# Two attention layers on one core: the order of small work around the projection streams

## The chip, the cores and the metric

The kernel runs on one core of a Trainium2 chip. The metric is the device time of one execution in microseconds (us), smaller is better. The engines are called TensorE (PE in the profile, PEld for its weight loads), VectorE (DVE), ScalarE (ACT), GpSimd (POOL) and SyncE (SP, which only issues transfers here). They run side by side; each takes its own instructions in order and waits for the others through semaphores.

## What is computed

Two layers, one after the other, on 8 images of 512 channels and 32 x 32 pixels, in float32. Cut to what matters:

```python
def layer(x, gn_w, gn_b, qkv_w, qkv_b, proj_w, proj_b, groups):   # groups: 8, then 32
    xn = group_norm(x, groups) * gn_w + gn_b
    q, k, v = split(einsum('oc,bcn->bon', qkv_w, xn) + qkv_b)     # 8 heads of 64
    attn = softmax(einsum('bhdi,bhdj->bhij', q, k) / 8)
    out = einsum('bhij,bhdj->bhdi', attn, v)
    return einsum('oc,bcn->bon', proj_w, out) + proj_b + x
```

## The kernel before

The work is cut into 16 **units**: unit u = 0 to 7 is layer 0 on image u, unit 8 to 15 is layer 1. In every unit two kinds of stage alternate.

**Projection streams.** A projection multiplies a 512 x 512 weight matrix with the 512 x 1024 image. It is done by a seven-product scheme in place of eight block products, on two levels: seven outer products k, in the order `ORDER = (1, 6, 2, 7, 5, 4, 3)` (L50), and in each of them seven inner **parts** j. The operands of the products are sums and differences of blocks, which have to be made first; the code calls this mixing. On the weights' side it is `mix_left` (L175): four operations on rows of 512 (outer) and four on 7 x 128 = 896 (inner). On the image's side it is `Right.mix`, `quarter` and `single` (L217 to L249). Weight mixtures are made once for each layer, stored as images in DRAM (`store_image`, L190) and loaded for each unit (`load_image`, L195).

`Stream.product` (L422) issues one outer product. Its parts 1, 6 and 5 accumulate into one small PSUM region called `one`; between them ScalarE copies that region to the main bank pair as a start value (`seed`, L443). So part 6 may only start when the copy behind part 1 has read `one`, part 5 when the copy behind part 6 has, and part 3 when the copy behind part 5 has written its quarter. Parts 4 and 3 are kept back as a **tail** and issued after part 1 of the next product. In steady state TensorE therefore runs 1', 4, 3, 6', 2', 7', 5', 1'', ... (dashes: the next products), and every copy has two parts to hide behind. The first product of a stream has no tail before it; there (`alone`, L449) part 7 is issued right behind part 1.

When a product is complete, `finish` **takes** it: VectorE adds the main bank pair to sums in SBUF, GpSimd adds the seventh part (`late`). The main pairs alternate, so the take of product n must be done before product n+2 can be seeded. After the take, `hook(sel, k)` runs whatever has been hung there with `at(sel, k, ...)` (L1011): mixing, loads, and work left over from the unit before. With "v,7" I mean the hook behind the take of product 7 of the v stream.

From unit 1 on a unit runs the streams v, q, k and then o (the output projection of the unit before). Work of the unit before that hangs in them: the transposed and reduced softmax sums of its last chunk (v,1 and v,2), their `reciprocals` (L894: five small VectorE operations, a transfer to DRAM and two broadcast transfers back), `divide` (L916), `add_bias` (L923), and the mixing of the attention output for the o stream (`ro.mix` and `o_part`, L1112). `o_part(5, ...)` and `o_part(1, ...)` run on VectorE, `o_part(2, ...)` and `o_part(4, ...)` on GpSimd.

Unit 0 makes v with full products (`make_values`, L697) and has no o stream. Beside its q and k streams VectorE mixes the first layer's weights as they arrive; those of o are `outer_o` and `inner_o` (L1091).

**Attention** (L782). 64 steps s, 8 chunks c of 8 steps t. In a step TensorE makes scores (L815, 8 records), ScalarE exponentiates them (L823), and the products with v of the step before follow (L843). VectorE adds up the exponentials (`summed`, L860). At t = 0 the chunk before is evacuated (a ScalarE copy L869, a VectorE add L870) and its sums transposed (L875), at t = 2 reduced (L883). The exponentials have five buffers. `at_step` (L1211) hangs the next unit's normalisation in the steps, by the tables USUAL and LATE (unit 0): statistics of x, means and variances (`norm`: small TensorE products into the other chunk's bank, read back by VectorE; the products of that chunk wait for the read-back through `free`), the scales, and their application on ScalarE (`apply`, which waits for the scales). `making` (L1220) mixes one weight matrix of layer 1 in each of units 1 to 4 on VectorE, two operations in each of chunks 1 to 4. `shadows` (L1249) are GpSimd operations that are made to follow a given sum[...].

Of the kernel before, what the change touches and what calls it, by code (L numbers as in the profile page):

```python
# [32 lines left out]
def fast_path(ctx, tc, x, qkv_wT, proj_wT, vecs, groups, out, flag):  # L33
# [5 lines left out]
    nc = tc.nc  # L39
# [3 lines left out]
    NT = N // P  # L43
# [367 lines left out]
    class Stream:  # L411


        def __init__(self, first):
            self.n, self.tail = first, None
# [6 lines left out]
        def product(self, a, b, keep, finish, tokens=False):  # L422
# [6 lines left out]
            def part(j, dst, tile_name, bank, start=False):  # L429
# [19 lines left out]
            alone = self.tail is None  # L449

            def apart():
                part(7, seventh, s, 1, not keep)

            def kept():
                on("ACT", nc.scalar.copy(late, seventh), s, 1)  # L455

            part(1, one, s, 0, True)
            if alone:
                apart()
            seed(q11, 0)  # L460
            if alone:
                kept()
# [4 lines left out]
            if not alone:  # L467
                apart()
                kept()
# [119 lines left out]
    def stream_values(stream, w, left, hook):  # L589
# [32 lines left out]
        for k in ORDER:  # L622

            def finish(main, m, late, k=k):
                steps[k](main, m, late)
                hook("v", k)

            stream.product(left.quarters(k), w.right.inner[k], k == 3, finish, True)
# [350 lines left out]
    def first_weights(after):  # L979
# [17 lines left out]
        "stats": (4, 5, 6, 7, 10, 11, 12, 13), "norm": (15, 20, 27, 30),  # L997
        "apply": (32, 33, 36, 38, 39, 41, 43, 44),
    }
    MAKE = {1: (1, "v"), 2: (1, "q"), 3: (1, "k"), 4: (1, "o")}  # L1000

    old = None
    for u in range(2 * B):
# [59 lines left out]
        if u == 0:  # L1063
# [28 lines left out]
            at("k", 2, partial(run, outer_o[:2]))  # L1092
            at("k", 7, partial(run, outer_o[2:]))
            at("k", 4, partial(run, inner_o[:2]))
            at("k", 3, partial(run, inner_o[2:]), partial(store_image, 0, "o", slot_q))
        else:
# [21 lines left out]
            at("v", 7, reciprocals)  # L1118
            at("v", 4, bias_2[0])
            at("v", 3, bias_2[1], o_rooms, partial(ro.mix, 0))  # L1120
            at("q", 1, divide)
            at("q", 6, bias[0])
            at("q", 2, bias[1])
            at("q", 7, partial(ro.mix, 1), o_part(2, 0, 1))
            at("q", 5, o_part(2, 1, 2))
            at("q", 4, partial(ro.mix, 3))
            at("q", 3, partial(ro.mix, 2))
            at("k", 1, o_part(1, 0, 2))
            at("k", 6, o_part(1, 2), o_part(2, 2, 3))
            at("k", 2, o_part(5, 0, 2), o_part(2, 3))  # L1130
# [405 lines left out]
```

## Time and profile before

| | us |
|---|---|
| three runs, median (lowest to highest) | 3202.29 (3200.21 to 3202.36) |
| the profiled execution: its time, its span from first to last instruction | 3201.04, 3199.3 |
| TensorE busy | 3174.4 (99%) |
| VectorE, ScalarE, GpSimd busy | 2682.8, 2045.5, 1223.6 |
| start of unit 0's attention, length of that attention | 88.08, 110.74 |
| unit 7: v stream; q, k and o streams; attention | 22.19, 64.72, 110.26 |
| v stream of units 1, 2, 4, 5 | 24.86, 22.56, 22.89, 22.85 |
| attention of units 1, 2, 3, 4 | 112.19, 111.36, 111.36, 111.35 |

The stage lengths are read from TensorE's timeline: from the first matmul of a stage to the first of the next one. A stream of v starts with the first matmul of 128 rows by 128 x 128 behind an attention, a q stream with the first of 128 x 256.

A timeline row has start, duration, engine, line, operation, output <- inputs, shape and count; what stands in brackets is how long the engine sat idle before it and what ended that. Neighbouring instructions of the same kind are merged (x4). Since matmuls are pipelined and their ends are modelled, this document measures TensorE from start to start.

### The profile page before, as it was taken

How to read it: one execution, taken by the hardware profiler on the slowest of the kernel's cores; microseconds unless marked ns; L12 is line 12 of the kernel's file. 1: busy time of each engine (PE TensorE's matmuls, PEld its weight loads, DVE VectorE, ACT ScalarE, POOL GpSimd, SP SyncE). 2: the span in 40 equal slices, each digit the busy share in tenths (PEclk: the TensorE clock that was granted, in tenths of full speed). 3: DMA queues.
4: the chain of work that ended last, by engine and by line, in shares of the span. 5: the costliest groups of instructions: out<-in, count | busy, mean ns of one | idle time of the engine just before them, and what ended most of it. 6: DMA issues, size and time to landing. Idle time of an engine off the chain costs nothing.

```text
span 3199.3 us, 63763 instructions
## 1 busy us (share of the span) xinstructions
PE 3174.4 (99%) x24272; PEld 2031.5 (63%) x24272; DVE 2682.8 (84%) x3172; ACT 2045.5 (64%) x3572; POOL 1223.6 (38%) x945
## 2 busy tenths in 40 slices
PE   9999999999999999999999999999999999999999
PEld 7466485664846659476584765847567485674843
DVE  7987978879788797887979879788797988879777
ACT  3665767667666676766667666676666766667664
POOL 4235171451714417154270533605336162351620
PEclk9999999999999999999999999999999999999999
DMA  4334342443424324243242331423314333243311
GB/s 173 108 120 136 118 141 88 167 137 115 150 81 169 120 74 148 82 130 120 63 161 79 119 127 56 167 79 122 119 58 165 90 127 102 83 149 91 131 62 49
DMA packets 155268, 365.78 MB, mean 114 GB/s; under 512 B 30160, under 2 KB 45776, under 8 KB 154960
## 3 DMA queue, kind: packets, MB, share of 16 engines
q1 hardware_dynamic: 154672, 361.53, 34.5%
q8 instruction: 195, 3.19, 0.4%
q14 instruction: 113, 0.93, 0.1%
q10 hardware_dynamic: 288, 0.13, 0.0%
HBM read 299.72 MB, written 59.77 MB: 112 GB/s over the span
## 4 chain that ended last, share of the span: by engine, by line
PE 85%; DVE 9%; issue 2%; DMA 1%; ACT 1%; SPq 1%; DVEq 0%; ACTq 0%
PE a L843 23%; PE s L815 22%; PE s L436 21%; PE a L436 16%; DVE acc L860 4%; PE a L815 1%; DMA lt<-red 1%; SPq L889 1%; DVE tr L875 1%; DVE red L883 1%; ACT a L444 0%; DVE ao L870 0%; ACT p L823 0%; PE s L761 0%; PE a L761 0%
## 5 line engine op out<-in xcount | busy, mean ns | idle before, releaser
L823 ACT ACTIVATE p<-s 128x1024 f32<-128x1024 f32 x976 | 997.8, 1024 | 525.7 <-PE s L815 492.6
L843 PE MATMUL a<-p,v 64*64 64x512 f32 x8192 | 1100.8, 589 | 2.7 <-ACT p L823 2.6
L815 PE MATMUL s<-q,k 64*64 64x512 f32 x7808 | 1058.9, 590 | 0.0
L860 DVE TENSOR_TENSOR acc<-acc,p 128x1024 f32<-128x1024 f32 x768 | 956.5, 1246 | 79.1 <-ACT p L823 37.3
L444 ACT COPY a<-s 128x256 f32<-128x256 f32 x1728 | 616.6, 358 | 336.6 <-PE s L436 224.4
L843 PEld LDWEIGHTS a<-p,v 64*64 64x64 f32 x8192 | 382.4, 131 | 500.9 <-ACT p L823 352.9
L815 PEld LDWEIGHTS s<-q,k 64*64 64x64 f32 x7808 | 384.7, 133 | 430.4 <-issue 430.4
L455 ACT COPY late<-s 128x256 f32<-128x256 f32 x432 | 160.9, 373 | 223.1 <-PE s L436 210.3
L436 PE MATMUL s<-k,w 128*128 128x256 f32 x672 | 195.1, 379 | 0.0
L1250 POOL TENSOR_TENSOR k<-xn 128x256 f32<-128x256 f32 x14 | 10.3, 734 | 444.3 <-PE s L815 283.9
L860 DVE TENSOR_TENSOR acc<-p,p 128x1024 f32<-128x1024 f32 x128 | 154.6, 1208 | 9.4 <-ACT p L823 9.4
L875 DVE STREAM_TRANSPOSE tr<-acc 128x1024 f32<-128x1024 f32 x128 | 157.9, 1234 | 0.0
L883 DVE TENSOR_REDUCE red<-tr 128x32 f32<-128x1024 f32 x128 | 154.0, 1203 | 0.0
L303 POOL TENSOR_TENSOR y<-var,half 128x4 f32<-128x4 f32 (+1 forms) x17 | 22.8, 1341 | 338.5 <-DVE var L301 338.5
L436 PE MATMUL a<-xn,w 128*128 128x256 f32 x492 | 146.3, 379 | 0.0
L436 PE MATMUL a<-xt,w 128*128 128x256 f32 x462 | 137.4, 379 | 0.0
L436 PEld LDWEIGHTS s<-k,w 128*128 128x128 f32 x672 | 125.6, 190 | 17.8 <-ACT a L444 0.4
L870 DVE TENSOR_TENSOR ao<-a,tmp 128x512 f32<-128x512 f32 x128 | 87.9, 686 | 50.9 <-ACT tmp L869 50.3
L489 POOL TENSOR_TENSOR q<-q,late 128x512 f32<-128x512 f32 x64 | 112.1, 1752 | 44.2 <-DVE q L560 29.7
L498 POOL TENSOR_TENSOR v<-v,late 128x512 f32<-128x512 f32 x60 | 89.1, 1494 | 58.4 <-DVE v L612 36.8
L436 PE MATMUL s<-xn,w 128*128 128x256 f32 x372 | 110.7, 379 | 0.0
L436 PE MATMUL s<-xt,w 128*128 128x256 f32 x372 | 110.6, 379 | 0.0
(264 smaller groups left out, 5067.6 us busy)
## 6 DMA issues: line engine op xcount, KB each, us to landing
w<-iq SPq DMA_DIRECT2D x105, 448.0 KB, 3.5
w<-ik SPq DMA_DIRECT2D x105, 448.0 KB, 7.1
w<-io SPq DMA_DIRECT2D x105, 448.0 KB, 3.6
w<-iv SPq DMA_DIRECT2D x98, 448.0 KB, 3.8
rb<-drec SPq DMA_DIRECT2D x128, 256.0 KB, 3.9
xn<-mid SPq DMA_DIRECT2D x36, 512.0 KB, 3.6
xn<-x_dram SPq DMA_DIRECT2D x32, 512.0 KB, 3.8
res<-x_dram SPq DMA_DIRECT2D x32, 512.0 KB, 6.1
```

Of the source, the lines that this page charges most:

```text
L436: nc.tensor.matmul(to, at, moving, start=start, stop=j != 1, skip_group_check=True),
L444: n = nc.scalar.copy(dst, one)
L455: on("ACT", nc.scalar.copy(late, seventh), s, 1)
L489: return nc.gpsimd.tensor_add(cols, cols, twice(late))
L498: return nc.gpsimd.tensor_add(cols, cols, parts)
L815: nc.tensor.matmul(bank[e * H : (e + 1) * H, j, :], w.k[pr][j * H : (j + 1) * H, t * P + e * H : t * P + (e + 1) * H], w.q[pr][j * H : (j ...
L823: exp = nc.scalar.activation(p, bank, AF.Exp, scale=SCALE)
L843: nc.tensor.matmul(banks[r][j * H : (j + 1) * H, :], w.v[rows, t, lo : lo + D], p[rows, j, :], start=(t == 0), stop=(t == NT - 1),)
L860: state["sums"].append(nc.vector.tensor_add(acc, state["first"] if t == 1 else acc, p))
L870: i1 = nc.vector.tensor_add(ao[:, pr, ts(qh, FD)], banks[1], tmp)
L875: nc.vector.transpose(tr, state["acc"].pop(c))
L883: nc.vector.tensor_reduce(red[:, :, qh, :], state["tr"].rearrange("p j (f i) -> p j f i", i=BL), AX.X, ALU.add)
```

## The change

Four edits.

1. `Stream.product` gets an argument `ahead`. In the v stream, from unit 1 on, the first product (k = 1) issues part 1 of the second product (k = 6) behind its own first seed; the second product then leaves its part 1 out. Part 7 of a stream's first product moves to where it is in all others, behind part 2.
2. The unit before's `reciprocals` move from v,7 to v,4 (the sixth take). `divide`, the two `add_bias` and the mixing for o move one hook later each, and the order of the outer mixings changes to 0, 3, 1, 2. On VectorE k,1 has `ro.mix(2)`, k,6 two of `o_part(1)`, k,2 its other two, k,7 two of `o_part(5)` in place of one, and k,4 two in place of one.
3. Layer 1's weights (units 1 to 4): the four outer operations and the first inner one at steps 1, 2, 3, 4 and 6 on VectorE (`MAKING`), the other three inner ones on GpSimd as shadows at steps 8, 16 and 24.
4. Unit 0: the mixing of o's weights moves one or two hooks later, its last two operations to steps 1 and 3 of the attention and the store to step 4. The tables LATE change: variances at step 23 in place of 27, scales at 26 in place of 30, application from 27 in place of 32. Unit 1's image mixing moves from ten VectorE operations at steps 43 to 60 to two on VectorE (35, 43) and nine GpSimd shadows (40 to 58).

```diff
-        def product(self, a, b, keep, finish, tokens=False):
+        def product(self, a, b, keep, finish, tokens=False, ahead=None):
...
-            part(1, one, s, 0, True)
-            if alone:
-                apart()
+            if not self.begun:
+                part(1, one, s, 0, True)
+            self.begun = ahead is not None
             seed(q11, 0)
-            if alone:
-                kept()
+            if ahead is not None:
+                part(1, sbank[i][:, 0, :FD2], f"s{i}", 0, True, *ahead)
             self.close()
             part(6, one, s, 0)
             seed(q21, 1)
             part(2, q11, m, 0)
-            if not alone:
-                apart()
-                kept()
+            part(7, seventh, s, 1, not keep)
+            on("ACT", nc.scalar.copy(late, seventh), s, 1)
             part(5, one, s, 0)
             seed(q12, 0)
...
-            stream.product(left.quarters(k), w.right.inner[k], k == 3, finish, True)
+            after = (left.quarters(6), w.right.inner[6]) if k == 1 else None
+            stream.product(left.quarters(k), w.right.inner[k], k == 3, finish, True, after)
...
     LATE = {
-        "stats": (4, 5, 6, 7, 10, 11, 12, 13), "norm": (15, 20, 27, 30),
-        "apply": (32, 33, 36, 38, 39, 41, 43, 44),
+        "stats": (4, 5, 6, 7, 10, 11, 12, 13), "norm": (15, 19, 23, 26),
+        "apply": (27, 28, 30, 31, 33, 35, 36, 38),
     }
+    MAKING = (1, 2, 3, 4, 6)
...
-            at("k", 2, partial(run, outer_o[:2]))
-            at("k", 7, partial(run, outer_o[2:]))
-            at("k", 4, partial(run, inner_o[:2]))
-            at("k", 3, partial(run, inner_o[2:]), partial(store_image, 0, "o", slot_q))
+            at("k", 7, partial(run, outer_o[:2]))
+            at("k", 4, partial(run, outer_o[2:]))
+            at("k", 3, partial(run, inner_o[:2]))
...
-            at("v", 7, reciprocals)
-            at("v", 4, bias_2[0])
+            at("v", 4, reciprocals, bias_2[0])
             at("v", 3, bias_2[1], o_rooms, partial(ro.mix, 0))
-            at("q", 1, divide)
-            at("q", 6, bias[0])
-            at("q", 2, bias[1])
-            at("q", 7, partial(ro.mix, 1), o_part(2, 0, 1))
-            at("q", 5, o_part(2, 1, 2))
-            at("q", 4, partial(ro.mix, 3))
-            at("q", 3, partial(ro.mix, 2))
-            at("k", 1, o_part(1, 0, 2))
-            at("k", 6, o_part(1, 2), o_part(2, 2, 3))
-            at("k", 2, o_part(5, 0, 2), o_part(2, 3))
-            at("k", 7, o_part(5, 2, 3), o_part(4, 0, 2))
-            at("k", 4, o_part(5, 3), o_part(4, 2))
+            at("q", 6, divide)
+            at("q", 2, bias[0])
+            at("q", 7, bias[1])
+            at("q", 5, o_part(2, 0, 1))
+            at("q", 4, partial(ro.mix, 3), o_part(2, 1, 2))
+            at("q", 3, partial(ro.mix, 1))
+            at("k", 1, partial(ro.mix, 2))
+            at("k", 6, o_part(1, 0, 2), o_part(2, 2, 3))
+            at("k", 2, o_part(1, 2), o_part(2, 3))
+            at("k", 7, o_part(5, 0, 2), o_part(4, 0, 2))
+            at("k", 4, o_part(5, 2), o_part(4, 2))
...
             if u == 0:
-                mixing.update(zip((44, 46, 47, 52, 54, 55, 59, 60), first_1 + first_6))
-                mixing[43], mixing[50] = partial(right.mix, 0), partial(right.mix, 1)
+                mixing[35], mixing[43] = partial(right.mix, 0), partial(right.mix, 1)
+                parts = zip((40, 40, 42, 48, 48, 50, 56, 56), first_1 + first_6)
+                parts = [*parts, *zip((58,), right.quarter((2, 3), (*halves(spare), halves(spare)[0]), nc.gpsimd))]
+                for step, part in parts:
+                    shadows.setdefault(step, []).append(part)
...
+                if make is not None:
+                    shadows.update((at, [part]) for at, part in zip((8, 16, 24), mix_left(left_slots[0], nc.gpsimd)[1][1:]))
...
             if make is not None:
-                if t in (3, 6) and c in range(1, 5) and 2 * (c - 1) + (t == 6) < len(making):
-                    making[2 * (c - 1) + (t == 6)]()
+                if s in MAKING:
+                    making[MAKING.index(s)]()
...
+            elif u == 0:
+                if s in (1, 3):
+                    inner_o[2 + s // 2]()
+                elif s == 4:
+                    store_image(0, "o", slot_q)
+                elif s == 5 * NT:
+                    store_image(0, "v", slot_v)
```

## The prediction

> **What bounds the kernel now.** I read the page's busy times first, then TensorE's timeline at the stage borders, then, wherever TensorE lost time there, the timelines of the engine it waited for.
>
> ```profile
> PE 3174.4 (99%) x24272; PEld 2031.5 (63%) x24272; DVE 2682.8 (84%) x3172; ACT 2045.5 (64%) x3572; POOL 1223.6 (38%) x945
> ```
>
> TensorE is the bound, so only its holes are worth anything. From start to start a part takes 0.4475 us in a v stream (4 records) and 0.4315 in q, k and o; an attention step takes 1.717. Against these rates all holes together come to some 50 us. Each edit can only win what its own holes hold. Unit 7, v stream:
>
> ```profile
> 1391.36 1.16 PE L436 MATMUL s<-w,xn 128*128 128x128 f32 x8
> 1392.57 0.71 PE L436 MATMUL s<-w,k 128*128 128x128 f32 x4
> 1393.12 0.61 PE L436 MATMUL a<-w,xn 128*128 128x128 f32 x4
> 1393.78 0.71 PE L436 MATMUL s<-w,k 128*128 128x128 f32 x4
> 1394.33 0.61 PE L436 MATMUL s<-w,xt 128*128 128x128 f32 x4
> ...
> 1408.33 0.59 DVE L899 TENSOR_REDUCE tot<-lt 32x64 f32<-32x256 f32 x1 [1.06 <-DMA lt<-red]
> 1409.89 0.67 DVE L542 TENSOR_TENSOR u_v<-a,u_v 128x512 f32<-128x512 f32 x1
> 1411.25 0.63 ACT L444 COPY a<-s 128x256 f32<-128x256 f32 x2 [0.67 <-DVE v L612]
> 1411.66 0.71 PE L436 MATMUL s<-w,spare 128*128 128x128 f32 x4 [0.19 <-ACT a L444]
> ```
>
> Parts 1 and 7 start at 1391.36, part 6 at 1392.57, part 5 at 1393.78: each pair that a ScalarE copy ties together is 1.21 apart. The part behind such a wait is followed by an interval of 0.55 in place of 0.4475. Lower down, VectorE waits 1.06 for the sums' transfer, does the reciprocals (1.63 to 1409.96), and takes product 5 late; the seed of product 3 waits for that, and TensorE starts 0.80 instead of 0.45 after its last part. The k stream of the same unit:
>
> ```profile
> 1446.89 0.68 DVE L409 TENSOR_TENSOR oa<-ot 128x512 f32<-128x512 f32 x1
> 1447.05 1.65 POOL L489 TENSOR_TENSOR k<-k,late 128x512 f32<-128x512 f32 x1
> 1447.60 1.64 DVE L409 TENSOR_TENSOR ob<-ot,oa 128x512 f32<-128x512 f32 x1
> 1449.17 1.40 DVE L532 SCALAR_TENSOR_TENSOR u_k<-a,step_vec,u_k 128x512 f32<-128x512 f32 x2
> 1450.49 0.67 DVE L409 TENSOR_TENSOR ob<-ot,ob 128x512 f32<-128x512 f32 x1
> 1450.65 1.66 POOL L489 TENSOR_TENSOR u_k<-u_k,late 128x512 f32<-128x512 f32 x1 [0.26 <-DVE u_k L532]
> 1451.33 0.69 DVE L542 TENSOR_TENSOR u_k<-a,u_k 128x512 f32<-128x512 f32 x1 [0.17 <-PE a L436]
> ```
>
> Of two mixings in a row, the second takes 1.64 because GpSimd's add gets in between. Last, unit 0's k stream, a window of it (its third figure from the end is the granted clock), and its attention:
>
> ```profile
> 77.72 1.42 DVE L409 TENSOR_TENSOR w<-w 128x512 f32<-128x512 f32 x2 [4.51 <-DMA w<-proj_wT_dram]
> 80.30 0.70 PE L436 MATMUL s<-xr,ot 128*128 128x256 f32 x2 [2.37 <-ACT a L444]
> ```
>
> ```profile
> 82.00:85.00 3.00, 3.00 (x8) 2.36 (x7) 3.00 (x5) 1.40 (x4) 0.19 (x1) 0.50 0.02 5
> ```
>
> ```profile
> 128.45 3.86 DVE L860 TENSOR_TENSOR acc<-acc,p 128x1024 f32<-128x1024 f32 x3
> 131.44 1.13 PE L843 MATMUL a<-p,v 64*64 64x512 f32 x8
> ```
>
> VectorE waits for the raw weights of o until 77.72 with takes queued behind them; TensorE idles 2.37 and then has a granted clock of 0.50.
>
> [...] GpSimd's 128 x 512 add takes 1.27 alone and 1.65 here, VectorE's mixing 0.68 and 1.64. [...] Here 2.37 us of idle were enough once, and 1.94 (unit 1's start) were not. [...]
>
> **1. Ahead part: +1.6 us.** Before, in part starts from the first one: 1 at 0, 7, 6 at 1.21, 2 at 1.76, 5 at 2.42, 1' at 2.97, 4, 3 at 3.86, 6' at 4.31. After: 1 at 0, 1' at 0.45, 6 at 1.21, 2 at 1.76, 7 at 2.21, 5 at 2.66 (its copy was ready at 2.42), 4 at 3.10. Part 3 needs the copy behind 5, so 2.66 + 1.21 = 3.87 instead of 3.55; 6' at 4.42. One hole is filled; the hole between 5 and 3, which 1' filled before, opens. Net 4.42 - 4.31 = 0.105 in 15 units. Bounds: -0.4 a unit (a hole filled and none opened) and +0.2.
>
> **2. Reciprocals: v gains, k loses.** With them gone from v,7 the take of 5 begins at about 1408.5, when TensorE is done with it; behind the take of 4 (1411.8 to 1413.0) they end at 1414.5, before the take of 3 is due (1414.9). The v stream becomes 22.13 - 0.35 + 0.105 = 21.88. The 15 v streams before add up to 337.0 (22.1 to 22.9, unit 1 24.86), after to 328.2: **-8.8**, item 1 included. This takes in unit 1's late start (1.94 and 0.45, because VectorE was 8.3 us behind at the end of unit 0) and units 2, 4 and 5, where making and a slow sums' transfer had cost 0.4 to 0.8 more. In each q stream 0.1 goes (the 0.55 behind the wait). On SP the two broadcasts move from 1412.5 to about 1417.0 and the loads of k's images behind them likewise; the last of those landed at 1425.67, so about 1430, due at 1434. The broadcasts land at about 1421.8 (3.8 and 4.3 each), and `divide` at q,6 is reached at about 1422.0: covered by a hair, and with 0.6 left after its own 1.2 until the next take is due. `add_bias` on ScalarE comes after it by a product. Nothing.
>
> The price is at k,7. Up to there VectorE's queue keeps its shape: k,1 has 1.2 for 1.4, k,6 and k,2 two mixings as before, each second one behind GpSimd's add. At k,7 there are now two: the first as above 1450.49 to 1451.16, then GpSimd's add to 1452.3, then the second to 1452.85. The take of 5 starts at 1452.77 in place of 1451.33. From its start to the dependent part it is 1.77 in the v case above (1409.89 to 1411.66), 1.79 with k's rows; so part 6 of product 3 starts at 1454.56 instead of 1454.15. Stall 0.41 plus 0.11 behind it, 0.52. Less 0.1 in q: 0.415 x 15 = **+6.2**. The takes of 4 and 3 come late as well, by my count within their allowance of about 1.0, the last by only 0.2. Bounds: 0[...] to 1.8 a unit (rival below).
>
> **3. Making: -5.2.** Units 1 to 4 take 112.19, 111.36, 111.36 and 111.35 for attention, the units without making 110.26. In chunk 0 sums leave 0.4 to 0.55 free a step, and VectorE idles 1.82 before the first evacuation (303.97 in unit 1); four mixings of 0.60 and one of 1.0 leave it about 1.1 behind at step 7, which that idle swallows. The raw weights landed at 286.99, step 1 is at 292.7. GpSimd's three take 2.10 each, as the same shadows do in unit 0,[...]. Sum of the four excesses: 1.93 + 1.10 + 1.10 + 1.09 = 5.2. Bounds: 3 to 5.2.
>
> **4. Unit 0: -4.2 and +4.4.** With o's mixing behind k,7 the take of 7 runs at 74.95; the mixing still waits to 77.72 and ends at 79.14; the take of 5 starts at 79.06 and holds part 6 of product 3 from 80.79 to 80.85. The 2.5 and the half clock's 1.4 go, attention starts at 83.9 in place of 88.08. But VectorE moves up only 2.9 (fourth sum at 94.9, before 97.79), so it is 1.3 further behind TensorE. The read-back of the variances, now at step 23, follows sum 23, which starts at 131.09 and ends at 132.31 (the row x3); its result is due for step 24's products, which ran at 131.44 (last row). That is 132.48 - 131.44 = 1.04 late, with the 1.3 above 2.35. Before, the read-back stood at step 27 with a chunk to spare. The scales at 26 come behind sum 26, and the application at 27, one step later and not two, waits for them on ScalarE with exponential 28 queued behind: without contention 1.4 of stall, with GpSimd's shadow of step 24 over sum 25 2.5; I take 2.2. Step 35 has a bias and an application together, 0.3 of stall, for the 0.45 that step 33 had. 2.35 + 2.2 - 0.15 = 4.4. Bounds 0 to 7.4 (half clock after both, 1.4 each).
>
> **Sum.** -8.8 + 6.2 - 5.2 - 4.2 + 4.4 = -7.6. The profiled span of 3199.3 becomes 3191.7, its time of 3201.04 (1.7 outside the span) 3193.4. The median of the runs is 1.25 above the profiled one: 3202.3 - 7.6 = **3194.7**.
>
> **Rivals.** (a) [...]no k stall: 15 x 0.52 = 7.8 less, 3186.9. For: the queue may drift.[...] Chance 0.10. (b) VectorE isn't behind in unit 0 and both statistics stalls stay away: 3190.3. Chance 0.15. (c) Those stalls bring the half clock twice: +2.8, 3197.5. The gap at 77.9 to 80.3 is for it, unit 1's is against. Chance 0.15. (d) [...] Then the take of 5 starts 1.3 later, the k stall is 1.8, 15 x 1.3 = 19.5 more: 3214. It turns the total to slower than +0.2% from 0.93 a unit on.[...] Chance 0.06. That edit 1 does nothing but shift its hole is in the forecast.
>
> **Chances.** Forecast 0.54. A measurement tells some 0.2%, 6.4 us, from no change, that is 3195.9. The forecast lies 1.2 inside; two thirds of it count as faster, 0.36. With (a) and (b) 0.61; within 0.33 (0.18 and (c)); slower 0.06. Range: from (a), a little further for the ahead part's bound, 3185, to (c) and the worst of the late k takes, 3199.5; (d) is left out.
>
> **What would show it.** Right: in v the 1.21 pairs are 1 to 6 and 5 to 3, v streams of about 21.9; reciprocals without a wait for lt; in k the take of 5 1.4 late, streams q to o of about 65.1; attention of units 1 to 4 near 110.3; unit 0's attention from about 84 and some 4 us longer, with products waiting for `var` and ScalarE for `shift`. Wrong: v streams that don't shrink, a k stream without a hole, or unit 0's attention no longer than before.

## The result and the profile after

| | before | after |
|---|---|---|
| median of 20 runs each (lowest to highest), us | 3202.09 (3199.69 to 3205.05) | 3197.15 (3196.19 to 3199.5) |
| ratio after to before | | 0.9986, 95% interval 0.9979 to 0.9993 |
| profiled execution: its time, its span | 3201.04, 3199.3 | 3197.46, 3195.5 |

The change gains 4.9 us in the medians and 3.8 in the profiled spans; the forecast was 7.6, or 3194.7 us. The time lies in the stated range and on the side of the forecast, but part of the gain, in the profiled spans half of it, is missing. (Medians and spans differ: the forecast took the median to be 1.25 above the profiled time, and it is 1.05 above it before and 0.31 below it after.) The first line of the page of after:

```profile
PE 3170.3 (99%) x24272; PEld 2016.2 (63%) x24272; DVE 2707.5 (85%) x3152; ACT 2041.8 (64%) x3572; POOL 1257.3 (39%) x965
```

TensorE is still the bound. Line numbers of after are 8 or 9 lower from about line 450 on (L843 is now L835, L542 is L533).

**v stream.** TensorE's timeline at the start of unit 7's v stream, columns as before:

```profile
1384.20 0.71 PE L436 MATMUL s<-w,xn 128*128 128x128 f32 x4
1384.75 0.61 PE L436 MATMUL s<-w,xt 128*128 128x128 f32 x4
1385.51 0.68 PE L436 MATMUL s<-w,k 128*128 128x128 f32 x4
...
1386.92 0.61 PE L436 MATMUL s<-w,k 128*128 128x128 f32 x4
1387.37 0.61 PE L436 MATMUL a<-w,k 128*128 128x128 f32 x4
1388.03 0.71 PE L436 MATMUL a<-w,xn 128*128 128x128 f32 x4
```

Rows one to three are parts 1, 1' and 6: 6 starts 1.31 behind 1. The last three are 5, 4 and 3: 3 starts 1.11 behind 5. So there is a hole ahead of part 6 and a new one ahead of part 3, as forecast (there 1.21 each, the sum is the same). The list of VectorE's waits has the reciprocals waiting for the sums' transfer (us in total, times, longest), before and after:

```profile
DVE tot L899 <- DMA lt<-red: 31.4, 23, 3.7
DVE tot L891 <- DMA lt<-red: 12.4, 11, 3.7
```

Before, 15 of the waits, 21.0 us, stand in the 15 v streams. After, none does; ten stand in attentions and one behind the last.

**k stream** of unit 7, all engines:

```profile
1443.09 1.65 POOL L480 TENSOR_TENSOR u_k<-u_k,late 128x512 f32<-128x512 f32 x1 [0.27 <-DVE u_k L523]
1443.64 1.64 DVE L409 TENSOR_TENSOR ob<-ot,oa 128x512 f32<-128x512 f32 x1
1445.21 0.68 DVE L533 TENSOR_TENSOR u_k<-a,u_k 128x512 f32<-128x512 f32 x1
...
1446.98 0.70 PE L436 MATMUL s<-spare,w 128*128 128x256 f32 x2 [0.21 <-ACT a L444]
```

The second mixing starts while GpSimd's add is under way (1443.09 to 1444.74) and takes 1.64, where the one ahead of that add, at 1442.93, takes 0.68; only then comes the take of product 5 (L533), and TensorE starts part 6 of product 3 at 1446.98, 0.80 behind its part before (1446.18) where 0.43 is the rule. In the kernel before there was no such row.

**Unit 0's attention**, first VectorE, ScalarE and TensorE in one timeline, then the windows behind it (the third figure from the end is the granted clock):

```profile
129.11 1.09 PE L835 MATMUL a<-p,v 64*64 64x512 f32 x8 [2.14 <-DVE var L301]
...
136.17 0.16 DVE L318 TENSOR_TENSOR shift<-vec,ms 128x4 f32<-128x4 f32 x1
136.37 0.81 ACT L322 ACTIVATE xn<-xn,shift,scale 128x512 f32<-128x512 f32 x1 [2.51 <-DVE shift L318]
...
138.24 0.66 PE L835 MATMUL a<-p,v 64*64 64x512 f32 x4 [2.03 <-ACT p L815]
```

```profile
138.00:140.00 2.00, 1.76 (x12) 0.75 (x16) 1.88 (x2) 1.70 (x3) 0.00 (x0) 0.71 0.03 8
140.00:142.00 2.00, 2.00 (x13) 0.68 (x9) 1.63 (x3) 0.49 (x1) 0.00 (x0) 0.50 0.00 0
```

Products wait 2.14 for `var`, ScalarE waits 2.51 for `shift` with the next exponential queued behind, and for this TensorE waits 2.03. Behind the second wait the granted clock is 0.50 for 3.41 us, from 138.82 to 142.23.

Where the 3.8 us of the spans come from, stage by stage from TensorE's starts:

| stage | forecast | measured |
|---|---|---|
| start of unit 0's attention | -4.2 | -4.53 (83.55), of which unit 0's q and k streams -4.18 |
| unit 0's attention | +4.4 | +6.13 (116.87) |
| the 15 v streams | -8.8 | -9.3 (21.80 each, 22.0 to 22.1 in units 10 to 12) |
| the 15 groups of q, k and o streams | +6.2 | +8.5 (65.2; 65.4 in units 2, 8 and 9; 66.02 in unit 10) |
| attention of units 1 to 4 | -5.2 | -5.1 (110.26 to 110.35) |
| the rest (most of it behind unit 15's attention) | 0 | +0.5 |
| sum | -7.6 | -3.8 |

The other 0.35 of the first row lies ahead of the q stream, which starts between 45.05 and 46.63 in the profiles here though nothing ahead of it was changed.

So the theory: v, making and unit 0's k stream earn what was forecast; it is lost again at k,7 and at two waits of unit 0's attention; the first edit alone is worth nothing. Rivals: the first edit pays for part of it; the k stall is only a sign of a VectorE that is late everywhere; the loss is in late transfers. All times below are medians, to be held against 3197.15 for the changed kernel; ratios are to the kernel before on the same chip. The median of the kernel before differs by up to 0.5 between these chips, so a difference of that size says nothing. Stage lengths are those of one profiled execution each.

### The profile page after: what moved, and what is told of

It reads as the page before. It is cut to its first block, busy times and chain, and to the rows that moved or that the text cites. A ratio compares the mean times of both kernels' runs of the same rounds, so it can differ in the third digit from the quotient of the medians.

```text
span 3195.5 us, 63766 instructions
## 1 busy us (share of the span) xinstructions
PE 3170.3 (99%) x24272; PEld 2016.2 (63%) x24272; DVE 2707.5 (85%) x3152; ACT 2041.8 (64%) x3572; POOL 1257.3 (39%) x965
## 4 chain that ended last, share of the span: by engine, by line
PE 93%; DVE 4%; ACT 1%; issue 1%; DMA 0%; POOL 0%; SPq 0%; ACTq 0%; DVEq 0%; POOLq 0%
PE a L835 27%; PE s L807 25%; PE s L436 22%; PE a L436 16%; PE a L807 1%; DVE acc L852 1%; DVE ob L409 1%; ACT a L444 1%; DVE u_k L523 1%; PE s L753 0%; PE a L753 0%; PE a L409 0%; DVE oa L409 0%; DVE k L562 0%; DVE u_k L533 0%
## 5 line engine op out<-in xcount | busy, mean ns | idle before, releaser
L835 PE MATMUL a<-p,v 64*64 64x512 f32 x8192 | 1098.2, 590 | 4.2 <-DVE var L301 2.1
L835 PEld LDWEIGHTS a<-p,v 64*64 64x64 f32 x8192 | 379.9, 131 | 505.0 <-ACT p L815 353.4
L807 PEld LDWEIGHTS s<-q,k 64*64 64x64 f32 x7808 | 377.9, 133 | 438.0 <-issue 438.0
L480 POOL TENSOR_TENSOR q<-q,late 128x512 f32<-128x512 f32 x64 | 98.4, 1537 | 62.8 <-ACT a L444 45.4
```

The lines of the kernel that those rows point to most:

```text
L480: return nc.gpsimd.tensor_add(cols, cols, twice(late))
L807: nc.tensor.matmul(bank[e * H : (e + 1) * H, j, :], w.k[pr][j * H : (j + 1) * H, t * P + e * H : t * P + (e + 1) * H], w.q[pr][j * H : (j ...
L835: nc.tensor.matmul(banks[r][j * H : (j + 1) * H, :], w.v[rows, t, lo : lo + D], p[rows, j, :], start=(t == 0), stop=(t == NT - 1),)
```

## Experiments

**Second mixing at k,7 taken away.** The same operations, one hook further apart:

```diff
-            at("k", 7, o_part(5, 0, 2), o_part(4, 0, 2))
-            at("k", 4, o_part(5, 2), o_part(4, 2))
+            at("k", 7, o_part(5, 0, 1), o_part(4, 0, 2))
+            at("k", 4, o_part(5, 1, 3), o_part(4, 2))
+            at("k", 3, o_part(5, 3))
```

> The changed kernel with one o_part(5) operation at k,7 as before, two at k,4 and the last at k,3; the same operations in all. Theory (the second mixing at k,7 waits behind GpSimd's add and makes the take of product 5 late): the hole before part 6 of product 3 of the k stream goes, the q, k and o streams together fall from 65.2 to about 64.65 a unit, 15 times 0.5 less: 3189.7 us. Rival (the late take of k is only where a general lateness of VectorE shows, carried over from the reciprocals and divide moved behind it): the hole moves to the next product, where the mixings now stand (part 6 of o's first product), the streams stay at 65.0 or more and the time at 3195 to 3199.

Measured: 3190.26 us, 0.9962 (0.9948 to 0.9976). Thirteen of fifteen groups of q, k and o streams are back at 64.73, the value of the kernel before; units 10 and 15 have another hole, told below. In unit 7's timeline the take of 5 stands right behind the one mixing and waits for TensorE, not the other way round:

```profile
1441.37 0.68 DVE L409 TENSOR_TENSOR oa<-ot 128x512 f32<-128x512 f32 x1
1441.53 1.65 POOL L480 TENSOR_TENSOR u_k<-u_k,late 128x512 f32<-128x512 f32 x1 [0.27 <-DVE u_k L523]
1442.23 0.69 DVE L533 TENSOR_TENSOR u_k<-a,u_k 128x512 f32<-128x512 f32 x1 [0.19 <-PE a L436]
```

The hole doesn't move to the o stream, so the doubling is its whole cause: 6.9 us in the medians.

**A third mixing at k,7.**

```diff
-            at("k", 7, o_part(5, 0, 2), o_part(4, 0, 2))
-            at("k", 4, o_part(5, 2), o_part(4, 2))
+            at("k", 7, o_part(5, 0, 3), o_part(4, 0, 2))
+            at("k", 4, o_part(5, 3), o_part(4, 2))
```

> The changed kernel with three o_part(5) operations at k,7 and one at k,4, in place of two and two: one suspected cost more, the same operations in all. Theory ([...]GpSimd's own mixings there come after): the third follows the second at once, the take of product 5 starts 0.68 later, the stall before part 6 of product 3 grows from 0.36 by 0.68, q, k and o streams 65.9: 3207.4 us. Rival[...]: 1.3 or more instead of 0.68, streams of 66.5 or more, 3216 us or more. Second rival (the take of 5 isn't what stalls there): streams stay within 0.2 of 65.2, 3197 to 3200 us.

Measured: 3213.46 us, 1.0036 (1.0023 to 1.005); streams of 66.33, 1.13 more a unit, where 0.68 or 1.3 had been expected. The timeline shows what lies between:

```profile
1450.45 1.18 POOL L409 TENSOR_TENSOR xt<-ot 128x256 f32<-128x256 f32 x1
1451.07 1.10 DVE L409 TENSOR_TENSOR ob<-ot,ob 128x512 f32<-128x512 f32 x1
1451.70 1.05 POOL L409 TENSOR_TENSOR xt<-ot,xt 128x256 f32<-128x256 f32 x1
1452.09 0.68 DVE L533 TENSOR_TENSOR u_k<-a,u_k 128x512 f32<-128x512 f32 x1
```

GpSimd's first mixing of that hook starts while VectorE's second (1449.39 to 1451.03) is still under way, and VectorE's third then takes 1.10 instead of 0.68. So the take of 5 starts 2.70 behind the second mixing's start, where it is 1.57 in the changed kernel: the 1.13 of the streams. GpSimd's second mixing doesn't get ahead of the take. So what the prediction's rival (d) has, time lost to GpSimd's own mixings, is seen with a third mixing, 0.42 beside one GpSimd operation. With two it isn't: in the changed kernel GpSimd's first starts at 1444.70 and VectorE's second at 1443.64.

**The first edit undone.** Part 7 of the first product stands behind part 1 again and the second product keeps its own part 1:

```diff
-            if not self.begun:
-                part(1, one, s, 0, True)
-            self.begun = ahead is not None
+            part(1, one, s, 0, True)
+            if alone:
+                apart()
             seed(q11, 0)
-            if ahead is not None:
-                part(1, sbank[i][:, 0, :FD2], f"s{i}", 0, True, *ahead)
+            if alone:
+                kept()
...
```

> The changed kernel without its first edit: the second product of v keeps its own first part, part 7 of a stream's first product stands behind part 1 again. The rest of the change is kept. Theory (the first edit fills one hole and opens another, 0.1 worse in a unit): the v streams go from 21.80 to about 21.70, the time is 3195.6 us, 1.6 less than the changed kernel, at any rate between 1 more and 3 less. Rival (the first edit earns the 0.76 of the hole that it fills and the rest of the v stream's gain is smaller than thought): v streams of 22.3 or more, 3204 us or more.

Measured: 3194.34 us, 0.9976 (0.9966 to 0.9986); v streams of 21.73 in units 2 to 15 against 21.80. In a unit the edit costs 0.07 (forecast 0.105), 1.0 us in all. The three longer v streams of units 10 to 12 are 21.73 here as well, which is 0.8 more; so with the edit the v streams are 1.7 longer in sum, and the forecast was 1.6. The median falls by 2.8; what the rest of that is was not settled. The rival, that the edit earns what it fills, falls.

**Part 3 of the first product one part later.** If the first edit only moves a hole, a part between 4 and 3 should close the new one. First try:

```diff
             if ahead is not None:
                 part(1, sbank[i][:, 0, :FD2], f"s{i}", 0, True, *ahead)
-            self.close()
+            if split:
+                self.tail(False)
+            else:
+                self.close()
             part(6, one, s, 0)
             seed(q21, 1)
+            if split:
+                fourth, self.tail = self.tail, None
+                fourth(True)
```

(Not shown: where `split` is set, and the tail cut in two. `split` is true in the product whose part 1 was issued ahead; `tail(False)` issues part 4, `tail(True)` part 3 and the finish.)

> The changed kernel with one part moved: at the second product of v, whose first part has been issued ahead, its part 6 goes between parts 4 and 3 of the first product, so that the copy behind part 5 has two parts to hide behind; the first product is taken one part later. Theory (what the first edit opened is the hole between parts 5 and 3): counted in part starts, 5 at 2.66, 4 at 3.11, part 6 of the second product at 3.55, part 3 at 4.00 and the next at 4.45 where the changed kernel has 4.87; v streams from 21.80 to 21.4, 15 times 0.4 less: 3191 us. Rival (the 0.76 comes from elsewhere, such as VectorE's take of the first product being late or the weight loads of part 3): the hole stays before part 3 or moves to the next seed, v streams stay at 21.7 or more and the time within 1.5 us of 3197.2.

Measured: 3200.9 us, 0.9995 (0.9987 to 1.0004), v streams of 22.14. Neither side was right: TensorE now waits ahead of part 6 of the second product.

```profile
1388.93 0.61 PE L436 MATMUL a<-w,k 128*128 128x128 f32 x4
1389.18 0.91 ACT L444 COPY a<-s 128x256 f32<-128x256 f32 x3
1389.96 0.68 PE L436 MATMUL s<-w,k 128*128 128x128 f32 x4 [0.42 <-ACT a L444]
```

The three copies are the seed behind part 5, then the second product's first seed, then the seed behind part 4. The part that the second one copies had been there since about 1387, some 2 us, but that seed was written behind the one for part 5, and it ran behind it. So the second try also issues this seed ahead, right behind the part that it copies:

```diff
+            if not split:
+                seed(q11, 0)
-            seed(q11, 0)
             if ahead is not None:
                 part(1, sbank[i][:, 0, :FD2], f"s{i}", 0, True, *ahead)
+                n = nc.scalar.copy(apair[1 - i][:, 0, :FD2], sbank[i][:, 0, :FD2])
...
```

> As the run with part 6 of the second product between parts 4 and 3, and now the second product's first seed (ScalarE's copy of the part that was issued ahead) also stands ahead, right behind that part, instead of behind the seed of part 5. Theory (in the earlier run part 6 of the second product waited 0.42 for exactly that copy, which stood third in ScalarE's queue): part starts 1 at 0, 6 at 1.31, 5 at 2.72, 4 at 3.17, 6 of the second product at 3.62, 3 at 4.07 and the next at 4.51 where the changed kernel has 4.83; v streams 21.80 to 21.5, 15 times 0.3 less, 3192.5 us. Rival (VectorE takes the first product later, and this sets the next product but one): v streams of 21.7 or more and 3196 to 3200.

Measured: 3190.77 us, 0.9964 (0.9951 to 0.9978), v streams of 21.48 in all fifteen units, 5.6 less in sum. Parts 5, 4, 6', 3 and 2' start at 1385.17, 1385.62, 1386.07, 1386.52 and 1386.96: all at the even pace of 0.45. What the first edit had left open was the hole between 5 and 3, and it closes.

**The reciprocals alone back at v,7.**

```diff
-            at("v", 4, reciprocals, bias_2[0])
+            at("v", 7, reciprocals)
+            at("v", 4, bias_2[0])
```

> The changed kernel with the reciprocals alone back at v,7; divide, add_bias and the mixings stay where the change put them. Theory (the reciprocals stood between TensorE and the take of product 5, and nothing else held v): v streams from 21.80 back to about 22.15, with VectorE waiting for lt there again, q, k and o streams unchanged at 65.2: 15 times 0.35 more, 3202.4 us. Rival (VectorE now comes to v less late than before, so that the transfer of the sums has landed by then, and the v gain came from making and unit 0 rather than from the move): v streams of 21.9 or less, 3198.5 us or less.

Measured: 3204.41 us, 1.0008 (1.0 to 1.0016); v streams of 22.18 to 22.95, on average 0.53 longer, q, k and o as in the changed kernel but for unit 10 (65.23). Unit 7:

```profile
1403.84 0.60 DVE L891 TENSOR_REDUCE tot<-lt 32x64 f32<-32x256 f32 x1 [1.48 <-DMA lt<-red]
1405.40 0.67 DVE L533 TENSOR_TENSOR u_v<-a,u_v 128x512 f32<-128x512 f32 x1
1407.17 0.71 PE L436 MATMUL s<-w,spare 128*128 128x128 f32 x4 [0.20 <-ACT a L444]
```

The wait for the sums' transfer is there again, the take of 5 late behind it and TensorE behind that. The move earns most of the v streams' gain: undone, it gives back 7.9 of the 9.3 in the v streams, 7.3 in the medians. A VectorE that comes to v less late doesn't help there, it waits longer for the transfer: 1.48 here in unit 7, 1.06 in the kernel before.

**Making of layer 1's weights as before.** Two operations in each of chunks 1 to 4, all on VectorE:

```diff
-                if s in MAKING:
-                    making[MAKING.index(s)]()
+                if t in (3, 6) and c in range(1, 5) and 2 * (c - 1) + (t == 6) < len(making):
+                    making[2 * (c - 1) + (t == 6)]()
```

The three GpSimd shadows go.

> The changed kernel with the old making in units 1 to 4: two operations in each of chunks 1 to 4, all on VectorE, none as GpSimd shadows; everything else as changed. Theory (VectorE is full in chunks 1 to 4 and every mixing there ends as a wait of TensorE): the attention of units 1 to 4 goes from 110.3 back to 112.2 and 111.4 three times, in sum 5.2 more, and with VectorE late at the attention's end up to 0.4 in the v streams of units 2 to 5: 3202.4 to 3204 us. Rival (unit 1's 112.2 and the 111.4 of the others came from VectorE's late start out of unit 0 and from the reciprocals, which are gone): attention of units 1 to 4 under 110.8, 3199 us or less.

Measured: 3202.41 us, 1.0002 (0.9993 to 1.001); attention of units 1 to 4 is 112.29, 111.37, 111.38 and 111.37, together 5.3 longer. Only unit 2's v stream grows (22.28). In unit 1 ScalarE waits for a buffer of exponentials until VectorE has added them up, and TensorE waits 0.91 for ScalarE:

```profile
366.48 1.94 ACT L815 ACTIVATE p<-s 128x1024 f32<-128x1024 f32 x2 [1.83 <-DVE acc L852]
367.65 1.09 PE L835 MATMUL a<-p,v 64*64 64x512 f32 x8 [0.91 <-ACT p L815]
```

The third edit's term holds to 0.1.

**Unit 0's table.** Three versions, since the first two each missed a wait. In all three the outer mixings for unit 1 (35 and 43 in the changed kernel) move along, which the diff doesn't show. First: variances at 25, scales at 27, application from 30.

```diff
-        "stats": (4, 5, 6, 7, 10, 11, 12, 13), "norm": (15, 19, 23, 26),
-        "apply": (27, 28, 30, 31, 33, 35, 36, 38),
+        "stats": (4, 5, 6, 7, 10, 11, 12, 13), "norm": (15, 19, 25, 27),
+        "apply": (30, 31, 33, 36, 38, 39, 41, 42),
```

> The changed kernel with unit 0's table LATE put later again: variances at step 25 in place of 23 (a whole chunk before the bank is used again), scales at 27, application at 30, 31, 33, 36, 38, 39, 41, 42, and the first outer mixing at 37 in place of 35. Theory (the loss in unit 0 comes from the two waits at steps 24 and 29 and the half clock behind them): unit 0's attention falls from 116.87 to between 110.5 and 111.5, no row with idle time for var or for ScalarE's wait for shift, granted clock 1.00 throughout; 3191.5 us, that is 5.6 less than the changed kernel. Rival (VectorE is behind in unit 0 because of the nine more GpSimd operations and the mixing of o's weights at steps 1 and 3, and TensorE loses the time wherever it next needs VectorE): the waits move to other steps, attention stays above 114 and the time within 2 us of the changed kernel's 3197.2.

Measured: 3193.11 us, 0.9974 (0.9965 to 0.9983); attention 112.39. Both old waits and the half clock are gone, but there is a new row:

```profile
129.49 0.22 PE L283 MATMUL a<-e,gmat 64*64 64x4 f32 x2 [1.87 <-DVE ao L862]
```

The variances' own matmul waits for the evacuation of chunk 2, which is issued at step 24 and which VectorE does over two steps late. Second: the whole table of before, variances at 27, scales at 30, application from 32, outer mixings at 39 and 45.

> The changed kernel with the whole table LATE of the kernel before (variances at step 27, scales at 30, application from 32) and the outer mixings at 39 and 45, as the application needs; the rest of the fourth edit stays. The run with variances at step 25 lost 2.14 at TensorE's own variance product, which waits there for the evacuation of the chunk before, issued one step earlier and late on VectorE. Theory (in unit 0 the time goes where something on TensorE's or ScalarE's path is asked of VectorE within two steps, VectorE being two steps behind): with three steps between evacuation and variances, and as much for scales, nothing waits: unit 0's attention 110.7 to 111.2 as in the kernel before, against 116.87; 3191.2 us. Rival (VectorE and GpSimd have more to do in unit 0 now, and it is paid anyway): attention stays at 112.3 or more, 3193 or more.

Measured: 3194.25 us, 0.9977 (0.9968 to 0.9985); attention 112.58, unit 1's v stream 22.24. These are the numbers of the rival there. Now the application is early again:

```profile
143.53 0.16 DVE L318 TENSOR_TENSOR shift<-vec,ms 128x4 f32<-128x4 f32 x1
...
143.73 0.81 ACT L322 ACTIVATE xn<-xn,shift,scale 128x512 f32<-128x512 f32 x1 [2.09 <-DVE shift L318]
```

In the kernel before the same table cost 0.14 at this place: there shift was ready 56.9 behind the attention's start, here it is 59.0. Third: variances at 27, scales at 29, application at 33, 36, 38, 39, 41, 43, 44 and 46.

> The changed kernel with both waits of unit 0 given room: variances at step 27 (three steps behind the evacuation), scales at 29, application from 33 (33, 36, 38, 39, 41, 43, 44, 46), outer mixings at 39 and 47. In the run with the table of before, scale and shift were ready at 143.7, 59.0 after the attention's start, and ScalarE's application at step 32 had asked for them 2.1 earlier; in the kernel before they were ready at 56.9. Theory (VectorE is two steps behind TensorE all through unit 0's attention since TensorE starts it 3.5 to 4.5 earlier, and only distance in the table helps): no hole of over 0.6 in unit 0's attention, length 110.3 to 110.9, 3191.0 us. Rival (the lateness grows with the nine GpSimd operations and the two mixings, and shows at the next dependent step, or at the start of unit 1's v stream as in the run before, 22.24): attention of 112 or more, or unit 1's v stream of 23 or more, 3193 us or more.

Measured: 3193.06 us, 0.9972 (0.996 to 0.9983). The attention is 110.29, without a hole, but unit 1's v stream is 23.77: the rival's sign. The rival is right on where the time goes: VectorE is behind, and what isn't paid at a wait inside the attention is paid at its end. From the start of unit 0's q stream to the end of unit 1's v stream the kernel before takes 177.8, the changed one 176.7 and the three tables 172.2, 172.9 and 172.1. The first and the third are alike, in the medians too. So of the 6.1 that unit 0's attention has lost, a table wins back three to four and a half (2.9 to 4.1 in the medians).

**Divide one product later.**

```diff
-            at("q", 6, divide)
-            at("q", 2, bias[0])
-            at("q", 7, bias[1])
-            at("q", 5, o_part(2, 0, 1))
+            at("q", 2, divide)
+            at("q", 7, bias[0])
+            at("q", 5, bias[1], o_part(2, 0, 1))
```

> The changed kernel with divide at q,2 in place of q,6, the two add_bias at q,7 and q,5, the rest as it is. In the changed kernel's trace one q stream (unit 10) has a hole of 0.68 because divide waits 0.42 for the broadcasts; two other runs have it in units 10 and 15. Theory (divide at q,6 is covered by a hair and some transfers miss it): no hole of over 0.3 in any q stream; about 0.8 less, 3196.4 us. Rival (the whole miss against the forecast, 2.5 us, comes from late broadcasts in many units): 3194.7 us or less. Second rival (the later mixings miss their own due times): holes in the o stream, 3199 us or more.

Measured: 3196.01 us, 0.9982 (0.9975 to 0.9989). Unit 10's streams fall from 66.02 to 65.23 and no q stream has a hole of over 0.3. In the changed kernel VectorE waits there 0.42 for the broadcasts, does `divide` in 2.00 instead of 1.22 (GpSimd is in an add from 2007.47, 1.27 long), and TensorE waits 0.52. One unit in fifteen: 0.8 us. In the medians it is 1.1, and 0.7 when each kernel is held against the kernel before on its chip.

```profile
2007.81 2.00 DVE L910 SCALAR_TENSOR_TENSOR ao<-ao,rb 128x1024 f32<-128x1024 f32 x1 [0.42 <-DMA rb<-drec]
2010.90 0.70 PE L436 MATMUL s<-k,w 128*128 128x256 f32 x2 [0.52 <-ACT a L444]
```

The other profiles with `divide` at q,6 and the reciprocals at v,4 have such a hole in one or two units, the one with a third mixing in none. So one profile without a hole is not enough to call the new place safe.

**Three repairs together**: the third table, one mixing at k,7, part 3 later with its seed ahead.

> Three repairs of the changed kernel together: table with variances at 27, scales at 29 and application from 33; one o_part(5) operation at k,7, two at k,4, one at k,3; part 6 of the second product of v between parts 4 and 3 with its seed ahead. If they are independent, as their places are (unit 0's attention, the k streams, the v streams), their gains add up: 6.2, 7.0 and 6.0 less than the changed kernel's 3197.2, so 3178 us, ratio 0.9925 to the kernel before. Rival (VectorE, relieved in one place, is the bound in the next: the shorter v and k streams make it late at the start of the attention): a sum of 14 or less, 3183 us or more.

Measured: 3180.3 us, 0.9931 (0.9918 to 0.9945), faster than both kernels. Apart the three gain 4.1, 6.9 and 6.4, that is 17.4, together 16.9: they add up but for half a microsecond. One of them does have a price in a new place: unit 1's v stream takes 25.53. The seed that stands ahead needs the bank pair of the last chunk, and in unit 1, where VectorE comes late out of unit 0, ScalarE waits 3.19 for the evacuation and TensorE 2.16 for ScalarE. Behind that TensorE is slow: the next two parts start 0.86 apart (199.86 and 200.72) in place of 0.45, which by the 3.41 us that half clock lasts in the changed kernel is estimated at 1.7 more:

```profile
198.63 0.36 ACT L456 COPY a<-s 128x256 f32<-128x256 f32 x1 [3.19 <-DVE ao L874]
199.31 0.75 PE L436 MATMUL s<-w,k 128*128 128x128 f32 x4 [2.16 <-ACT a L444]
```

The profiled execution, 3182.89, is the longest of the five; whether the others have this isn't known. Units 6 and 15 have the hole of `divide`, which isn't repaired here. The gain is 2.3 short of the expected one, and larger than the rival's 14. The first table with the other two was not tried.

## Why the prediction was right and where it was wrong

**What held.** TensorE was the bound, and each edit was worth its own holes. The step on the ahead part: a hole filled, another opened; the two came out as 1.31 and 1.11 and not as 1.21 twice. Part 6' starts 4.38 behind part 1 (forecast 4.42), and 4.31 without the edit, so the size was 0.07 a unit instead of 0.105. The step on the v streams: -9.3 for -8.8, 21.80 for 21.88. Making: -5.1 for -5.2, and undoing it gives 5.3 back. Unit 0's k stream: -4.18 for -4.2, though the terms named for it, 2.5 and 1.4, make only 3.9: the half clock there lasted from 81.74 to 85.15, 3.41 us at 0.50, which costs 1.7 and not 1.4. The figures that the k step was built on hold in the changed kernel too: VectorE's mixing takes 0.68 where it starts ahead of GpSimd's add (1442.93 for 1443.09) and 1.64 behind it (1443.64).

**The k term was too small.** Forecast 6.2, measured 8.5. The stall was sized right, 0.37 and 0.10 behind it for 0.52. But "less 0.1 in q" failed: with the second mixing gone, q, k and o are at 64.73 just as in the kernel before, so q had nothing to win. That is 0.47 instead of 0.415 in each unit, 0.8 in all. Another 0.8 is `divide`, which the prediction costed at nothing, "covered by a hair": in one unit the cover was missing. The last 0.6 are units 2, 8 and 9, whose streams are 0.2 longer. In unit 8 it is a term that the prediction had at nothing, the late take of product 3, which it counted within its allowance "by only 0.2": two mixings at k,4 take 1.22 and 1.75 and the take behind them starts at 1648.80, with a hole of 0.13 and 0.10 behind it. In unit 9 the stall at k,7 is 0.60 in place of 0.37, and in unit 2 there is another of 0.18 two parts further on; why there isn't settled.

**The unit 0 term was too small by the half clock.** The two waits had been put at 2.35 and 2.2; they cost 2.41 and 2.23. What came on top is 1.7 of half clock, the prediction's rival (c), once instead of twice, and 1.7 instead of 1.4 each. (The 0.45 that the prediction sees at step 33 before is 0.14 there; the rest, some 0.3, stands at the attention's start.) In the changed kernel and in the run with part 3 later and its seed ahead it follows the second wait (there the granted clock is 0.74 and 0.50 in the 2 us from 138 and from 140), and the attention is 116.9. In the runs without the first edit, with the reciprocals back and with a third mixing it follows the first wait (0.57, 0.57 and 0.61 in the 4 us from 130). Then VectorE catches up, the second wait shrinks to 0.54 and the attention is 115.2. That is what the forecast had without any half clock, by luck. In the run without the second mixing at k,7 the first wait took 3.73 in place of 2.41, with 3.0 of half clock (0.58 in the 4 us from 130, 0.50 and 0.63 in the 2 us from 134 and from 136) and no second wait, 117.15. A row of the run without the first edit, for the first kind:

```profile
131.63 2.01 PE L816 MATMUL s<-q,k 64*64 64x512 f32 x8
...
139.22 1.09 PE L844 MATMUL a<-p,v 64*64 64x512 f32 x8 [0.33 <-ACT p L824]
```

Scores that take 1.07 otherwise take 2.01 here; four steps later the second wait is reached and is small. The first edit touches neither gap; what the profiles show of the two stands in the last section. So 1.7 of the 3.2 between this profile's span and that of the changed kernel is the half clock's place.

**What wasn't seen.** The prediction read unit 0's price from its two waits. The table runs show that these are where a debt of VectorE is called in. In the run with the table of before TensorE starts the attention 3.4 earlier than in the kernel before (84.67 for 88.08), but VectorE has shift only 1.3 earlier (143.7 for 145.0), and moving the calls later moves the payment to the start of unit 1. The trace of that run tells where this comes from. The nine GpSimd operations are no part of it, since the first of them starts at 159.88. VectorE's first sum starts 5.40 behind the attention's start, against 5.73 before, but the two mixings now at steps 1 and 3 take 1.08 each: about the 2.1 by which shift is later, seen from the attention's start. What the nine cost later, at the start of unit 1, was not tried apart. From unit 0's q stream to the end of unit 1's v stream the change gains 1.1 us over the kernel before; the best tables found gain 5.6 and 5.7.

**The rivals.** (a), no k stall, and (b), no waits in unit 0, fall by the rows above. (c) came true by half. (d), GpSimd's own mixings ahead of VectorE's second, falls for two mixings; with a third, VectorE's last takes 1.10 in place of 0.68, with GpSimd's beside it. The measured 3197.15 lies nearer to the 3197.5 of (c) than to the forecast, and part of that is luck: (c) gave 2.8 to half clock alone, while the profile has 1.7 of it, and the k term was 2.3 too small besides. It also lies behind the 3195.9 that the prediction took for the least that a measurement can tell; with 20 runs each the interval is 0.0007 to either side, so the gain of 0.14% is clear.

## What to carry to other kernels

Filling one hole of a chain with the part that covered another is worth nothing; it takes another part for the second hole, and a look at the queue of the engine that serves the chain, where a copy can be held by its place alone (TensorE waited 0.42 for one here). Of two mixings in a row on VectorE the second took 1.64 in place of 0.68 here, beside GpSimd's add, and one of them moved a hook further took 6.9 us off the whole: spread such operations. When a fix lets the bound engine start earlier, ask whether its feeder starts earlier as well; if not, the wait comes back at the next dependent step. And when two profiles differ by some 2 us in a stage that no edit touched, look at the clock before looking at the code: here full clock followed a gap of 2.14 in one profile, and half clock, 1.7 more, a gap of 2.15 in another.

## What the runs showed of the hardware

**What half clock followed.** In the kernel before, half clock lasts 3.41 us, from 81.74 to 85.15, behind TensorE's gap of 2.37; in the changed kernel it lasts 3.41 us behind the second gap of unit 0's attention. Cut into stretches of that length, counted from the start of half clock, the two gaps of the changed kernel look like this; a row has the stretch, its length, TensorE's busy time and instructions, the granted clock, and the share and GB/s of the DMA engines:

```profile
125.17:128.58 3.41, 1.80 (x18) 1.00 0.31 117
128.58:131.99 3.41, 2.88 (x28) 1.00 0.49 154
...
135.41:138.82 3.41, 1.38 (x16) 1.00 0.00 0
138.82:142.23 3.41, 3.41 (x24) 0.50 0.02 5
```

The first gap has 1.61 of idle time in one of the stretches and 0.53 in the next, and the clock stays full. The second has 2.03 in the stretch right ahead of half clock. In the kernel before, 1.97 of the 2.37 lie in the 3.41 us right ahead of it.

The length of a gap alone doesn't tell. Without the first edit half clock follows a first gap of 2.15: the granted clock is 0.58 and 0.57 in the 2 us from 130 and from 132, and 1.00 from 134. At full clock TensorE goes on behind 2.14 in the changed kernel, behind 2.06 (ahead of 145.59) in the run with the table of before, where the clock is 1.00 from 138 to 148, and behind 1.77 at the start of unit 1 in the kernel before, where it is 1.00 from 203 to 209. In the run without the second mixing at k,7 half clock lasts 6.8 behind the gap of 3.7, by the granted clocks given above. These figures alone don't show what decides between full and half clock.

**Weight loads behind a wait.** In unit 7's v stream of the kernel before, the load of the weights starts 0.11 ahead of its matmul where TensorE hasn't waited (1393.01 for 1393.12, 1394.22 for 1394.33), and together with it behind a wait (both at 1392.57 and at 1393.78). The interval after such a part is longer by the same 0.1: 0.55 in place of 0.4475.
